# Attention followed by a learned density, one core: the density's last product moved from VectorE to ScalarE and POOL, with new pacing and a reordered tail

## The chip, the cores and the metric

The kernel runs on one core of one Trainium2 chip. Its time is device microseconds of that core. A core has TensorE (PE; its weight loads are listed apart as PEld), VectorE (DVE), ScalarE (ACT), GpSimd (POOL) and SyncE (SP, which issues DMAs). Each engine executes its own queue in order; a waiting instruction holds up all that stand behind it on the same engine.

## What is computed

The input `x` has 8 images of 192 channels and 64 x 64 pixels, in float32. Two layers follow each other, each added to its input. Both normalize first: the mean and variance of each group of 6 channels over all pixels of an image.

```python
# layer 0: attention over the 4096 pixels of an image
q = prelu(conv1x1(x, w1, b1), a1)        # 24 channels
k = prelu(conv1x1(x, w2, b2), a2)        # 24 channels
v = prelu(conv1x1(x, wa, ba), aa)        # 192 channels
score = softmax(einsum('bnc,bcm->bnm', q, k), axis=2)
out = einsum('bnm,bmc->bnc', score, v)
# layer 1: a small network for each channel, widths 1, 3, 3, 3, 1
for i in range(4):
    logits = einsum('cij,cjn->cin', softplus(ms[i]), logits) + bs[i]
    if i < 3:
        logits = logits + tanh(fs[i]) * tanh(logits)
# lower and upper are these logits for x - 0.5 and x + 0.5
sign = -sign(lower + upper)
likelihood = max(abs(sigmoid(sign * upper) - sigmoid(sign * lower)), 1e-6)
```

The density of an image (layer 1) can begin only when the attention output of that whole image is there, since its norm is taken over all of it.

## The kernel before

**The loop.** The attention of all images is one stream of 1,024 steps, 128 for an image: 8 blocks of 512 queries (`n`), and 16 steps of 256 keys each in a block. In a step TensorE makes the scores of the next step (L780), the products from which the row maximum of a later block is taken (L708, 22 steps ahead), and adds `e` times `v` to the block's accumulator (L795). ScalarE takes the exponential (L784), VectorE reduces the maximum (L716). At the end of a block the accumulator is divided, transposed through the tiles `o` and added to `xc` (`finish`, L806 to L840); after the last block of an image its norm follows (`norm_end`), a chain of small products and small VectorE instructions that ends in `wn` and `bn` (L503, L506).

**Beside it.** Keys, queries and values of the next image are made by jobs that take free steps; `keys` (L609) writes both keys and queries to a tile `kq`, from which two DMAs take them away. The density of an image runs beside the attention of the next one.

**The density.** It is cut into 12 units for an image: 2 column parts `c`, 3 channel groups `g`, and `s` for lower and upper. A unit works on tiles of 128 x 1,024 in 17 shared buffers `d`. ScalarE makes tanhs (L1005 of the input, L1020 later ones) and the first term of each sum, with scale and bias (L1014, L1030); VectorE adds each further term by one instruction that multiplies by a number per partition and adds (L1037): 9 "mixes" into layer 1, 3 gates, 6 products of layer 2, 3 gates, and 2 products of the last layer, 23 in all. When both units of a pair (`c`, `g`) are done, `ending` (L1135) makes the likelihood and adds it to `xc`: in the loop with POOL (L1160, L1172, L1180, each on half the columns), near the end on VectorE alone (`alone`, L1187 to L1197), then the absolute value (L1205), the sum (L1209) and the stores (L1213).

**The order.** It is written out by a planner while the program is built. A step `t` is a slot in all queues; `at(t, fn)` puts work into a later slot. In each slot `density_step` (L1086) gives VectorE, ScalarE and TensorE a credit and lets the oldest three units issue instructions as long as there is credit, inputs were issued earlier, and enough buffers stay for older units (`need`, L1063). VectorE's credit per step in the loop is the work left, divided by the steps until 15 after the next image's end. `pool_step` (L1120) issues one POOL piece in a step, behind a one-column memset (`pause`, L1125) that waits for the last but one density product of VectorE, so that the piece starts near the reduce.

**The tail.** The density of the last image has no attention beside it. There the nine mixes and the linear terms of a unit go to TensorE, for all units but the first: for each of three outputs, 8 matmuls of 512 columns against diagonal matrices (L978) add up in PSUM; ScalarE takes the tanh from there (L986) and VectorE gates it (L996). The diagonals (27 from weights at L876, 9 from the norm at L882) are made by ScalarE after the loop. After the loop each slot has a credit of 4.15.

Of the kernel before, what the change touches and what calls it, by code (L numbers as in the profile page):

```python
# [9 lines left out]
F32 = mybir.dt.float32  # L10
# [7 lines left out]
def kernel(  # L18
# [590 lines left out]
    def keys(b, d, what, done):  # L609

        t = xi[what, b, d]
        c, h = divmod(d, 2)
        i = c % 2

        def make(pk, u):
            if b not in kt:
                kt[b] = kpool.tile([128, N // 4], F32, tag="k", name=f"k_{b}")
            write, read = spotted()
            for g in range(3):
                write(nc.tensor.matmul(  # L620
                    pk[:, 0:P], lhsT=wf[i, b][:, g, :], rhs=t[:, g, :],
                    start=g == 0, stop=g == 2,
                ))
            done()
            kq = work.tile([128, P], F32, tag="kq", bufs=3, name=f"kq_{b}_{d}")
            first, last = prelu(
                None, kq, pk[:, 0:P], wf["b", i, b], nslope[:, i : i + 1],
                [x[:, 0:P] for x in u], read,
            )

            def move():
                last()
                k, q = (slice(64 * j, 64 * j + 64) for j in (i, 1 - i))
                u = (c // 2) * F + h * P
                nc.sync.dma_start(out=kt[b][k, u : u + P], in_=kq[k])
# [170 lines left out]
    def finish(b, n, t):  # L806
        a = acc.pop((b, n))
        rc = small.tile([128, 4], F32, tag="rc", name=f"rc_{b}_{n}")
        o = [
            work.tile([128, 3, 2, R], F32, tag=f"o{k}", name=f"o{k}_{b}_{n}") for k in range(2)  # L810
        ]
        cell = {}

        def invert():
            nc.vector.reciprocal(rc, a[:, :, C])

        def evacuate(k):
# [14 lines left out]

        u = slice((n % 4) * 256, (n % 4) * 256 + 256)

        def residual():
            xcc = xc[b, n // 4]
            nc.vector.tensor_tensor(xcc[:, :, u], xcc[:, :, u], cell["po"][:, 0:3, :], ALU.add)

            at(now[0] + 1, stat, 1.3)

        def stat():
            for g in range(3):
                norm_stat((b, 1), 3 * n + g, xc[b, n // 4][:, g, u])
            if n == NB - 1:
                norm_end((b, 1), 3 * NB, now[0] + 1, lambda: density(b))

        def make(po, _):
            cell["po"] = po.rearrange("p a (j c) -> p (a j) c", j=2)
            return [(0, turn, 0.0, 0.0, 1.3), (1, residual, 1.0, 0.0, 0.0)]
# [12 lines left out]

    ACT_RATE = 2.9
    OTHER = 0.1
    COST = {"DVE": 1.22, "ACT": 1.23, "TANH": 1.05, "PE": 6.95}
    diag = []
    banks = deque()
    lower2 = mm.rearrange("p g n -> p (g n)")[:, 0:36].rearrange("p (s g i) -> p s g i", s=4, g=3)

    def diagonals(g):  # L870

        d = vtiles.pop(0).rearrange("p a b c -> p (a b c)")[:, 0 : 12 * 128]
        d = d.rearrange("p (k n) -> p k n", k=12)
        diag.append(d)
        for k in range(9):
            nc.scalar.activation(d[:, k, :], ident, AF.Copy, scale=lc[:, g, k : k + 1])  # L876

    def linear_diagonals(b):
        wn, bn = norms[b, 1]
        for g in range(3):  # L880
            for i in range(3):
                nc.scalar.activation(  # L882
                    diag[g][:, 9 + i, :], ident, AF.Copy, scale=wn[:, g, 1, i : i + 1]
                )

        for s in range(2):
            d, q = lower2[:, s], lower2[:, 2 + s]
# [14 lines left out]
    class Unit:  # L902
# [3 lines left out]
        def __init__(self, b, c, g, s):  # L906
# [1 line left out]
            self.at = {}  # L908
            self.buf = {}
            self.todo = {"DVE": deque(), "ACT": deque(), "PE": deque()}  # L910
            self.left = {"l": 6, "t": 9, "u": 0, "z": 1}
            self.held = {"l": 0, "t": 0, "u": 0, "z": 0}
            self.on_pe = b == B - 1 and c + g + s > 0
            add = self.add
            if self.on_pe:

                self.left.update(t=3, u=3)
                for i in range(3):
                    add("ACT", ("u", 0, i), [], self.tanh0, makes="u")
                for i in range(3):  # L920
# [25 lines left out]
            for i in range(3):  # L946
                add("DVE", ("gate", 2, i), [("t", 2, i)], self.gate, frees=[("t", 2, i)])
            add("ACT", ("l", 3, 0), [("gate", 2, 0)], self.scaled, makes="z")
            for j in (1, 2):
                add("DVE", ("add", 3, 0, j), [("gate", 2, j), ("l", 3, 0)], self.more)  # L950

        def add(self, eng, name, after, fn, makes=None, frees=()):
            self.todo[eng].append((name, after, fn, makes, frees))
# [95 lines left out]
        def more(self, k):  # L1049
# [4 lines left out]
                for q in range(3):  # L1054
                    self.give(("l", 1, q))
            if (n, j) == (3, 2):
                for q in range(3):
                    self.give(("l", 2, q))
                b, c, g, s = self.key
                if not any(u.key == (b, c, g, 1 - s) and u.todo["DVE"] for u in units):  # L1060
                    ending(b, c, g)

        def need(self):  # L1063
            most = dict(self.left, t=max(0, min(self.left["t"], 1 - self.held["t"])))
            return sum(most.values())

        def step(self, eng, t, older):
# [18 lines left out]
    def density_step(t, rate):  # L1086
        if units and t < last:

            left = sum(len(u.todo["DVE"]) for u in units if u.key[0] == units[0].key[0])
            rate = left * COST["DVE"] / max(1, (units[0].key[0] + 2) * IMG + 15 - t) + OTHER  # L1090
        act = ACT_RATE if t < last else rate

        for eng, most in (("DVE", rate), ("ACT", act)):
# [1 line left out]
            credit[eng] = min(credit[eng] + most, most + more)  # L1095
        credit["PE"] = min(credit["PE"] + rate, rate)
        for eng in ("ACT", "PE", "DVE"):
            order = list(range(min(3, len(units))))
            if len(units) == 2:

                order.sort(key=lambda n: -len(units[n].todo["DVE"]))
            for n in order:
                units[n].step(eng, t, list(units)[:n])
        for u in [u for u in units if not u.todo["DVE"]]:
            units.remove(u)

    def density(b):
        if b == B - 1:
            linear_diagonals(b)
        for c in range(2):  # L1110
            for g in range(3):
                for s in range(2):
# [22 lines left out]
    def ending(b, c, g):  # L1135
# [46 lines left out]
        def alone():  # L1182

            s = cell["s"]

            def first():
                nc.vector.tensor_tensor(s, z[0], z[1], ALU.add)  # L1187
                later(1, second, 0.0, 2.1)

            def second():  # L1190
                for i in range(2):
                    nc.scalar.activation(z[i], z[i], AF.Tanh, scale=0.5)
                later(1, third, 2.5)

            def third():
                nc.vector.tensor_tensor(z[0], z[1], z[0], ALU.subtract)
                nc.vector.scalar_tensor_tensor(z[0], s, 0.0, z[0], ALU.not_equal, ALU.mult)  # L1197
                bufs.extend((s, z[1]))
                later(1, size, 0.0, 1.1)
                later(2, store, 1.3)  # L1200

            later(1, first, 1.25)

        def size():
            nc.scalar.activation(z[0], z[0], AF.Abs, scale=0.5)  # L1205

        def store():
            x_ = xc[b, c][:, g, :]
            nc.vector.scalar_tensor_tensor(x_, z[0], 1e-6, x_, ALU.max, ALU.add)  # L1209
            bufs.append(z[0])  # L1210
            for i in range(2):
                k = i * N // 2 + c * 2 * F
                nc.sync.dma_start(  # L1213
                    out=ov[b, :, g, k : k + 2 * F], in_=x_[R * i : R * i + R]
                )
            if g == 2:
                xc.pop((b, c))
                free["xc"] += 1
# [135 lines left out]
    for t in range(last):  # L1354
        b = t // IMG
        if t % IMG == 0:
            within(b, t)
            if b + 1 < B:
                prepare(b + 1, t)
        now[0] = t  # L1360
        if t % STEPS == 0:
            homes[:] = [(turns[(t // STEPS + 1) % 2], [0, 0])]
# [8 lines left out]
        work_off(t, RATE - 1.215)  # L1371
    t = last
    homes[:] = [(turns[1], [0, 0])]
    for g in range(3):
        at(t + 4 + g, lambda g=g: diagonals(g))
    while due or units or jobs or loads:
        work_off(t, RATE)
        t += 1
# [1 line left out]

# [36 lines left out]
```

## Time and profile before

| | us |
|---|---|
| median of 3 runs | 4846.51 (4843.33 to 4850.05) |
| the profiled execution | 4845.56 |
| its span, first to last instruction | 4843.8 |
| busy: PE / PEld / DVE / ACT / POOL | 4656.6 / 3443.8 / 4260.6 / 3116.6 / 523.3 |

The page's groups of instructions, with the count, busy time, mean ns of one and the idle time before it:

```profile
L716 DVE TENSOR_REDUCE rm<-mx 128x1 f32<-128x1024 f32 x1002 | 1222.4, 1220 | 445.9 <-PE mx L708 440.8
L1037 DVE SCALAR_TENSOR_TENSOR d<-d,wsp,d 128x1024 f32<-128x1024 f32 x768 | 984.6, 1283 | 45.7 <-ACT d L1030 34.4
L1160 POOL TENSOR_TENSOR d<-d,d 128x512 f32<-128x512 f32 x80 | 173.1, 2164 | 0.7 <-issue 0.2
```

A busy time is a sum over the whole span and says nothing about which engine sets the pace of a stage; a busy TensorE is busy in the records also where its matmuls wait inside the pipeline. VectorE's large instructions have a mean of about 1.28 us, but the next one starts 1.2 us after: their ends overlap. The chain of work that ended last runs over PE for 79% of the span and over DVE for 14%.

### The profile page before, as it was taken

The page shows a single profiled execution, that of the slowest core. Times are in us where ns is not written, and L with a number is a line of the kernel's source. Part 1 is how long each engine was busy: PE and PEld are TensorE (multiplying, and loading weights), DVE is VectorE, ACT ScalarE, POOL GpSimd, SP SyncE. Part 2 cuts the span into 40 slices and gives each one's busy share as a digit, 9 for nine tenths or more (in the row PEclk, how much of TensorE's full clock was granted, in tenths as well). Part 3 has the DMA queues.
Part 4 walks back from the last instruction along what each step waited for, and adds up shares of the span by engine and source line. Part 5 has one row for each costly group of instructions (what it writes and reads, how often), then busy time and mean ns, then how long its engine had stood idle before and what let it go on. Part 6 is the DMA issues. An engine that isn't in the chain of part 4 may idle for free.

```text
span 4843.8 us, 68352 instructions
## 1 busy us (share of the span) xinstructions
PE 4656.6 (96%) x28384; PEld 3443.8 (71%) x28384; DVE 4260.6 (88%) x4378; ACT 3116.6 (64%) x3581; POOL 523.3 (11%) x506
## 2 busy tenths in 40 slices
PE   7999999999999999999999999999999999999496
PEld 5777777777777777777777777777777777777132
DVE  5433369999999999999999999999999999998887
ACT  2332247676767667777667766776777767777665
POOL 0000001111112111111111101111111111211000
PEclk9999999999999999999999999999999999999698
DMA  2101010001100111111110111110111100000000
GB/s 61 38 23 24 18 48 25 25 24 40 42 20 24 40 35 34 31 32 29 38 29 26 37 39 29 31 37 15 35 42 28 27 24 22 10 23 5 9 13 13
DMA packets 109163, 138.55 MB, mean 29 GB/s; under 512 B 17074, under 2 KB 82100, under 8 KB 108852
## 3 DMA queue, kind: packets, MB, share of 16 engines
q1 hardware_dynamic: 107616, 133.81, 11.0%
q8 instruction: 222, 3.64, 0.3%
q14 instruction: 89, 0.73, 0.1%
q10 hardware_dynamic: 1236, 0.37, 0.0%
HBM read 100.58 MB, written 29.36 MB: 27 GB/s over the span
## 4 chain that ended last, share of the span: by engine, by line
PE 79%; DVE 14%; ACT 4%; issue 1%; POOL 1%; DMA 0%; ACTq 0%; DVEq 0%; POOLq 0%
PE b L795 48%; PE sc L780 18%; DVE d L1037 9%; PE b L669 4%; DVE rm L716 3%; PE b L978 2%; PE b L620 1%; PE sc_tail L978 1%; PE mx_tail L978 1%; PE b L828 1%; ACT e L784 1%; PE mx L708 1%; ACT d L1005 1%; ACT d L1030 1%; ACT d L1020 1%
## 5 line engine op out<-in xcount | busy, mean ns | idle before, releaser
L795 PEld LDWEIGHTS b<-v,e 128*128 128x128 f32 x16384 | 2662.2, 191 | 779.1 <-issue 775.3
L795 PE MATMUL b<-v,e 128*128 128x193 f32 x16384 | 2966.5, 335 | 0.0
L784 ACT ACTIVATE e<-sc 128x1024 f32<-128x1024 f32 x1024 | 1044.9, 1020 | 1444.1 <-PE mx L708 1409.3
L716 DVE TENSOR_REDUCE rm<-mx 128x1 f32<-128x1024 f32 x1002 | 1222.4, 1220 | 445.9 <-PE mx L708 440.8
L780 PE MATMUL sc<-q,k 25*128 25x512 f32 x4096 | 1155.8, 640 | 22.4 <-ACT e L784 22.3
L708 PE MATMUL mx<-k,q 24*128 24x512 f32 x4008 | 1132.7, 641 | 14.1 <-DVE rm L716 13.8
L1037 DVE SCALAR_TENSOR_TENSOR d<-d,wsp,d 128x1024 f32<-128x1024 f32 x768 | 984.6, 1283 | 45.7 <-ACT d L1030 34.4
L1037 DVE SCALAR_TENSOR_TENSOR d<-d,lc,d 128x1024 f32<-128x1024 f32 x765 | 986.5, 1300 | 16.5 <-ACT d L1014 5.1
L1037 DVE SCALAR_TENSOR_TENSOR d<-d,tf,d 128x1024 f32<-128x1024 f32 x543 | 680.9, 1277 | 2.5 <-ACT d L1020 2.5
L1020 ACT ACTIVATE d<-d 128x1024 f32<-128x1024 f32 x543 | 568.0, 1053 | 65.3 <-DVE d L1037 64.7
L780 PEld LDWEIGHTS sc<-q,k 25*128 25x128 f32 x4096 | 306.4, 183 | 249.9 <-issue 189.1
L1125 POOL MEMSET pause<- 128x1 f32 x240 | 23.5, 98 | 3888.0 <-DVE d L1037 3888.0
L1030 ACT ACTIVATE d<-d,cb,wsp 128x1024 f32<-128x1024 f32 x351 | 433.4, 1235 | 2.3 <-DVE d L1037 1.7
L1005 ACT ACTIVATE d<-xc,bn,wn 128x1024 f32<-128x1024 f32 x288 | 353.6, 1234 | 12.2 <-DVE bn L506 11.4
L708 PEld LDWEIGHTS mx<-k,q 24*128 24x128 f32 x4008 | 299.9, 183 | 30.3 <-DVE rm L716 29.1
L1014 ACT ACTIVATE d<-xc,bn,wn 128x1024 f32<-128x1024 f32 x255 | 314.7, 1234 | 0.0
L1160 POOL TENSOR_TENSOR d<-d,d 128x512 f32<-128x512 f32 x80 | 173.1, 2164 | 0.7 <-issue 0.2
L1172 POOL TENSOR_TENSOR d<-d,d 128x512 f32<-128x512 f32 x80 | 167.3, 2092 | 0.4 <-issue 0.4
L1180 POOL TENSOR_TENSOR d<-d,d 128x512 f32<-128x512 f32 x80 | 161.7, 2021 | 1.9 <-ACT d L1030 0.3
L669 PE MATMUL b<-wv,xi 64*128 64x192 f32 x1344 | 139.5, 340 | 0.2 <-ACT pra L596 0.2
L669 PEld LDWEIGHTS b<-wv,xi 64*128 64x128 f32 x1344 | 106.5, 186 | 25.7 <-issue 20.2
L978 PE MATMUL b<-d,v 128*128 128x512 f32 x204 | 95.9, 622 | 17.1 <-ACT d L1005 17.1
(154 smaller groups left out, 2064.4 us busy)
## 6 DMA issues: line engine op xcount, KB each, us to landing
xi<-in_x_dram SPq DMA_DIRECT2D x280, 192.0 KB, 3.4
xc<-in_x_dram SPq DMA_DIRECT2D x64, 384.0 KB, 7.0
out_dram<-xc SPq DMA_DIRECT2D x96, 256.0 KB, 3.1
q<-qd SPq DMA_DIRECT2D x128, 128.0 KB, 2.6
k<-kq SPq DMA_DIRECT2D x64, 64.0 KB, 1.9
qd<-kq SPq DMA_DIRECT2D x64, 64.0 KB, 2.1
d<-in_x_dram SPq DMA_DIRECT2D x16, 192.0 KB, 4.6
d<-in_wat_dram ACTq DMA_DIRECT2D x2, 144.0 KB
```

The lines of the kernel that those rows point to most:

```text
L669: nc.tensor.matmul(pv[:, s, 0:C], lhsT=t[p, g, k * 128 : k * 128 + 128] if g < 3 else one_row[p], rhs=wf["v", b][p, g, :] if g < 3 else wf ...
L708: nc.tensor.matmul(sc[:, s, :], lhsT=tile_of(qt[b, n // 2], n, j)[r], rhs=kt[b][r, u : u + F], start=True, stop=True,)
L716: nc.vector.tensor_reduce(out=rowmax[b, n][:, j, k : k + 1], in_=sc, axis=AX.XY, op=ALU.max)
L780: nc.tensor.matmul(sc[:, s, :], lhsT=kt[b][r, k : k + 128], rhs=qt[b, n // 2][r, :, u : u + 256], start=True, stop=True,)
L784: return lambda: nc.scalar.activation(e, sc, AF.Exp)
L795: nc.tensor.matmul(a[:, j, 0 : C + 1], lhsT=e[:, s, j * 128 : j * 128 + 128], rhs=v[:, s, p % 4, :], start=p == 0 and s == 0 and j % 2 == ...
L978: nc.tensor.matmul(out[:, h, :], lhsT=diag[g][:, 3 * i + n - 1 if n else 9 + i, :], rhs=src[:, h * F : h * F + F], start=n == 0, stop=n == 3,)
L1005: nc.scalar.activation(self.buf[k], self.src(), AF.Tanh, bias=bn[:, s, g, 0, i : i + 1], scale=wn[:, g, 0, i : i + 1],)
L1014: nc.scalar.activation(self.buf[k], self.src(), AF.Identity, bias=bn[:, s, g, 1, i : i + 1], scale=wn[:, g, 1, i : i + 1],)
L1020: nc.scalar.activation(self.buf[k], self.buf["l", k[1], k[2]], AF.Tanh)
L1030: nc.scalar.activation(self.buf[k], self.buf["l", n - 1, 0], AF.Identity, bias=offset, scale=wsp[:, g, w : w + 1],)
L1037: nc.vector.scalar_tensor_tensor(dst, src, factor, dst, ALU.mult, ALU.add)
```

## The change

1. In units that do not use TensorE (now all units of the first seven images), the last layer's last product, `("add", 3, 0, 2)` on VectorE, becomes a copy with a scale on ScalarE into a buffer of its own (`plain`, kind `p`), and two POOL pieces that add its halves to the unit's result.
2. The credit of VectorE in the loop has a ceiling `MOST` of 3.3.
3. `need` counts the buffers of the last layer only when the second layer's last product has been issued.
4. `kq` goes from three buffers to two; the tiles `o` from one to two each.
5. The tail: the weights' diagonals are made one by one in the last steps of the loop; the norm's diagonals are spread over slots; until the last norm is there a slot's credit is 1.3; after the loop up to four units may issue; the first unit uses TensorE too; the last pair's ending works on halves and stores halves.

```diff
-            kq = work.tile([128, P], F32, tag="kq", bufs=3, name=f"kq_{b}_{d}")
+            kq = work.tile([128, P], F32, tag="kq", bufs=2, name=f"kq_{b}_{d}")
...
-            work.tile([128, 3, 2, R], F32, tag=f"o{k}", name=f"o{k}_{b}_{n}") for k in range(2)
+            work.tile([128, 3, 2, R], F32, tag=f"o{k}", bufs=2, name=f"o{k}_{b}_{n}") for k in range(2)
...
+    MOST = 3.3
...
-    def diagonals(g):
-
-        d = vtiles.pop(0).rearrange("p a b c -> p (a b c)")[:, 0 : 12 * 128]
-        d = d.rearrange("p (k n) -> p k n", k=12)
-        diag.append(d)
+    def diagonals(g, t):
+
+        def one(k):
+            if k == 0:
+                d = vtiles.pop(0).rearrange("p a b c -> p (a b c)")[:, 0 : 12 * 128]
+                diag.append(d.rearrange("p (k n) -> p k n", k=12))
+            nc.scalar.activation(diag[g][:, k, :], ident, AF.Copy, scale=lc[:, g, k : k + 1])
+
         for k in range(9):
-            nc.scalar.activation(d[:, k, :], ident, AF.Copy, scale=lc[:, g, k : k + 1])
+            at(t + k, lambda k=k: one(k), 0.0, 0.4)
...
-            self.on_pe = b == B - 1 and c + g + s > 0
+            self.on_pe = b == B - 1
...
-            for j in (1, 2):
-                add("DVE", ("add", 3, 0, j), [("gate", 2, j), ("l", 3, 0)], self.more)
+            add("DVE", ("add", 3, 0, 1), [("gate", 2, 1), ("l", 3, 0)], self.more)
+            if self.on_pe:
+                add("DVE", ("add", 3, 0, 2), [("gate", 2, 2), ("l", 3, 0)], self.more)
+            else:
+
+                add("ACT", ("p", 3, 2), [("gate", 2, 2), ("add", 3, 0, 1)], self.plain, makes="p")
...
+        def plain(self, k):
+            g = self.key[2]
+            src, dst, z = self.buf["l", 2, 2], self.buf[k], self.buf["l", 3, 0]
+            nc.scalar.activation(dst, src, AF.Copy, scale=wsp[:, g, 23:24])
+
+            def add(h):
+                n = slice(h * F, h * F + F)
+                if h == 1:
+                    at(now[0] + 1, lambda: self.give(k))
+                return nc.gpsimd.tensor_tensor(z[:, n], z[:, n], dst[:, n], ALU.add)
+
+            pieces.append(lambda: add(0))
+            pieces.append(lambda: add(1))
+            self.end()
...
         def need(self):
             most = dict(self.left, t=max(0, min(self.left["t"], 1 - self.held["t"])))
+            if ("add", 2, 2, 2) not in self.at:
+
+                most.update(z=0, p=0)
             return sum(most.values())
...
             rate = left * COST["DVE"] / max(1, (units[0].key[0] + 2) * IMG + 15 - t) + OTHER
+            rate = min(rate, MOST)
...
-            order = list(range(min(3, len(units))))
-            if len(units) == 2:
+            order = list(range(min(3 if t < last else 4, len(units))))
+            if len(units) == 2 and t < last:
...
         if b == B - 1:
-            linear_diagonals(b)
+            linear_diagonals(b, 0)
+            for g in (1, 2):
+                at(now[0] + 3 * g, lambda g=g: linear_diagonals(b, g), 0.0, 1.2)
+            at(now[0] + 1, lambda: tail(b), 2.2)
...
+            parts = halves if (b, c, g) == (B - 1, 1, 2) else [slice(0, 2 * F)]
...
+                diagonals(0, t + 93)
+                diagonals(1, t + 104)
+                diagonals(2, last - 11)
...
-    for g in range(3):
-        at(t + 4 + g, lambda g=g: diagonals(g))
     while due or units or jobs or loads:
-        work_off(t, RATE)
+
+        work_off(t, RATE if (B - 1, 1) in norms else 1.3)
         t += 1
```

More of the change, by code (lines that the diff above doesn't have):

```diff
@@ L868, with linear_diagonals, tail @@
     lower2 = mm.rearrange("p g n -> p (g n)")[:, 0:36].rearrange("p (s g i) -> p s g i", s=4, g=3)
-    def diagonals(g):
-        d = vtiles.pop(0).rearrange("p a b c -> p (a b c)")[:, 0 : 12 * 128]
-        d = d.rearrange("p (k n) -> p k n", k=12)
-        diag.append(d)
+    def diagonals(g, t):
[4 more added lines that the diff above has]
+            nc.scalar.activation(diag[g][:, k, :], ident, AF.Copy, scale=lc[:, g, k : k + 1])
         for k in range(9):
-            nc.scalar.activation(d[:, k, :], ident, AF.Copy, scale=lc[:, g, k : k + 1])
-    def linear_diagonals(b):
+            at(t + k, lambda k=k: one(k), 0.0, 0.4)
+    def linear_diagonals(b, g):
         wn, bn = norms[b, 1]
-        for g in range(3):
[L881 to L884, printed above, removed]
+        for i in range(3):
+            nc.scalar.activation(
+                diag[g][:, 9 + i, :], ident, AF.Copy, scale=wn[:, g, 1, i : i + 1]
+            )
+    def tail(b):
+        wn, bn = norms[b, 1]
         for s in range(2):
@@ L910, in __init__ @@
             self.todo = {"DVE": deque(), "ACT": deque(), "PE": deque()}
-            self.left = {"l": 6, "t": 9, "u": 0, "z": 1}
-            self.held = {"l": 0, "t": 0, "u": 0, "z": 0}
-            self.on_pe = b == B - 1 and c + g + s > 0
+            self.left = {"l": 6, "t": 9, "u": 0, "z": 1, "p": 1}
+            self.held = {"l": 0, "t": 0, "u": 0, "z": 0, "p": 0}
+            self.on_pe = b == B - 1
             add = self.add
             if self.on_pe:
-                self.left.update(t=3, u=3)
+                self.left.update(t=3, u=3, p=0)
                 for i in range(3):
@@ L1056, in more, with end, busy @@
             if (n, j) == (3, 2):
[L1057 to L1061, printed above, removed]
+                self.end()
[10 more added lines that the diff above has]
+            pieces.append(lambda: add(1))
+            self.end()
+        def end(self):
+            for q in range(3):
+                self.give(("l", 2, q))
+            b, c, g, s = self.key
+            if not any(u.key == (b, c, g, 1 - s) and u.busy() for u in units):
+                ending(b, c, g)
+        def busy(self):
+            return self.todo["DVE"] or self.todo["ACT"]
         def need(self):
             most = dict(self.left, t=max(0, min(self.left["t"], 1 - self.held["t"])))
+            if ("add", 2, 2, 2) not in self.at:
+                most.update(z=0, p=0)
             return sum(most.values())
@@ L1103, in density_step @@
                 units[n].step(eng, t, list(units)[:n])
-        for u in [u for u in units if not u.todo["DVE"]]:
+        for u in [u for u in units if not u.busy()]:
             units.remove(u)
@@ L1184, in alone @@
             s = cell["s"]
+            parts = halves if (b, c, g) == (B - 1, 1, 2) else [slice(0, 2 * F)]
             def first():
-                nc.vector.tensor_tensor(s, z[0], z[1], ALU.add)
+                for n in parts:
+                    nc.vector.tensor_tensor(s[:, n], z[0][:, n], z[1][:, n], ALU.add)
                 later(1, second, 0.0, 2.1)
             def second():
-                for i in range(2):
-                    nc.scalar.activation(z[i], z[i], AF.Tanh, scale=0.5)
+                for n in parts:
+                    for i in range(2):
+                        nc.scalar.activation(z[i][:, n], z[i][:, n], AF.Tanh, scale=0.5)
@@ L1193, in second @@
                 later(1, third, 2.5)
             def third():
-                nc.vector.tensor_tensor(z[0], z[1], z[0], ALU.subtract)
-                nc.vector.scalar_tensor_tensor(z[0], s, 0.0, z[0], ALU.not_equal, ALU.mult)
+                for n in parts:
+                    y = z[0][:, n]
+                    nc.vector.tensor_tensor(y, z[1][:, n], y, ALU.subtract)
+                    nc.vector.scalar_tensor_tensor(y, s[:, n], 0.0, y, ALU.not_equal, ALU.mult)
                 bufs.extend((s, z[1]))
-                later(1, size, 0.0, 1.1)
@@ L1200, in third, with size @@
-                later(2, store, 1.3)
+                later(1, lambda: size(parts), 0.0, 1.1)
+                later(2, lambda: store(parts), 1.3)
             later(1, first, 1.25)
[L1204 to L1209, printed above, removed]
-            bufs.append(z[0])
[L1211 to L1215, printed above, removed]
+        def size(parts=(slice(0, 2 * F),)):
+            for n in parts:
+                nc.scalar.activation(z[0][:, n], z[0][:, n], AF.Abs, scale=0.5)
@@ L1216, in store @@
+        def store(parts=(slice(0, 2 * F),)):
+            for n in parts:
+                x_ = xc[b, c][:, g, n]
+                nc.vector.scalar_tensor_tensor(x_, z[0][:, n], 1e-6, x_, ALU.max, ALU.add)
+                for i in range(2):
+                    k = i * N // 2 + c * 2 * F
+                    nc.sync.dma_start(
+                        out=ov[b, :, g, k + n.start : k + n.stop], in_=x_[R * i : R * i + R]
+                    )
+            bufs.append(z[0])
             if g == 2:
@@ L1359 @@
                 prepare(b + 1, t)
+            else:
+                diagonals(0, t + 93)
+                diagonals(1, t + 104)
+                diagonals(2, last - 11)
         now[0] = t
@@ L1373 @@
     homes[:] = [(turns[1], [0, 0])]
-    for g in range(3):
-        at(t + 4 + g, lambda g=g: diagonals(g))
     while due or units or jobs or loads:
-        work_off(t, RATE)
+        work_off(t, RATE if (B - 1, 1) in norms else 1.3)
         t += 1
```

## The prediction

> **What bounds the kernel now.** I read the page first, then a table of windows by image and for the tail, then the timeline where the table showed a loss. In the windows the columns after the length are the busy times of TensorE, its weight load, VectorE, ScalarE and POOL, each with a count, then the granted clock, the DMA share and GB/s.
>
> ```profile
> 88.90:632.00 543.10, 540.85 (x3458) 410.39 (x3456) 202.02 (x280) 163.89 (x214) 0.00 (x0) 1.00 0.10 25
> 1737.50:2293.90 556.40, 551.84 (x3484) 417.35 (x3482) 541.04 (x549) 392.40 (x452) 78.08 (x72) 0.99 0.13 32
> 4479.50:4531.30 51.80, 2.78 (x11) 2.14 (x10) 49.92 (x59) 33.35 (x56) 0.00 (x0) 0.53 0.04 10
> 4531.30:4586.70 55.40, 34.24 (x65) 14.21 (x66) 49.26 (x54) 42.09 (x45) 0.00 (x0) 0.76 0.04 10
> 4586.70:4807.30 220.60, 204.34 (x465) 88.28 (x463) 178.60 (x146) 141.84 (x132) 0.00 (x0) 0.98 0.04 10
> 4807.30:4843.80 36.50, 0.00 (x0) 0.00 (x0) 25.92 (x22) 14.05 (x13) 0.00 (x0) 0.54 0.11 29
> ```
>
> The first row is image 0's attention, with no density beside it: 543.1 us, TensorE full. The second is image 3's, with image 2's density: 13 us longer, and VectorE now full too (541 of 556). The loop's floor is TensorE. Timing the loop by the first score matmul of each step, a plain step takes 3.88 us (median and minimum of 675), one with value products 5.38, with keys 5.18, with the output transposes 4.54. The medians sum to 4,301 us; the real steps take **84 us more**: 1.6, 6.2, 13.6, 13.6, 13.2, 13.0, 13.0 and 9.9 us in images 0 to 7. That is all the loop can give back. Some 10 us of each 13 lie in steps 13 to 17, where the old density's due time, the new norm and the next image's statistics meet:
>
> ```profile
> 1809.08 2.67 DVE L1037 SCALAR_TENSOR_TENSOR d<-d,lc,d 128x1024 f32<-128x1024 f32 x2
> ...
> 1811.66 1.22 DVE L716 TENSOR_REDUCE rm<-mx 128x1 f32<-128x1024 f32 x1
> ...
> 1812.94 1.69 PE L708 MATMUL mx<-k,q 24*128 24x512 f32 x4 [2.77 <-DVE rm L716]
> ...
> 1814.56 5.52 PE L795 MATMUL b<-v,e 128*128 128x193 f32 x16
> ```
>
> VectorE reached this reduce late, TensorE stood 2.77 us, and its next 16 matmuls took 5.52 us where they usually take 2.88: the records show the granted clock at 0.5 from 1813.4 to 1820.2. Being late costs twice.
>
> The tail, from 4479.5 on, has four stages: norm of the last image (VectorE busy 49.9 of 51.8), start of TensorE's products, the steady products, the drain. The span ends 1.8 us inside the profiled 4845.56, which is 0.95 under the median.
>
> **The last product (84 units of images 0 to 6).** Removed: 84 L1037 instructions; two in a row take 2.60, so 1.2 start to start, 101 us in all or 14.4 per image. Added on ScalarE: 84 copies with a scale; not in the trace, between L1020 (1.05) and L1030 (1.24), I take 1.15 (two operands, no bias): 14 us an image, under ScalarE's 164 us of idle time an image. Exposed, it would cost those 14. Added on POOL: 168 half adds behind 168 pauses, 24 per image. Their price is the open question, since the adds can hold up VectorE:
>
> ```profile
> 1822.46 2.60 DVE L1037 SCALAR_TENSOR_TENSOR d<-d,lc,d 128x1024 f32<-128x1024 f32 x2
> ...
> 1823.91 2.27 POOL L1160 TENSOR_TENSOR d<-d,d 128x512 f32<-128x512 f32 x1
> ...
> 1825.19 1.22 DVE L716 TENSOR_REDUCE rm<-mx 128x1 f32<-128x1024 f32 x1
> ...
> 4410.14 2.21 POOL L1180 TENSOR_TENSOR d<-d,d 128x512 f32<-128x512 f32 x1
> ...
> 4411.14 3.61 DVE L1037 SCALAR_TENSOR_TENSOR d<-d,wsp,d 128x1024 f32<-128x1024 f32 x2
> ```
>
> In the first case the half add waits out the second product and then runs beside the reduce: both DVE rows keep their usual length. In the second no reduce follows, and two products take 3.61, 1.0 more. The Trainium skill ("SBUF — State Buffer", Who interferes with whom) says the shared port pair is an exclusive lock: a VectorE instruction with two SBUF inputs and a GpSimd one that reads SBUF block each other wholly. By that rule alone all 168 adds collide at 1.0 each, 168 us against 101 saved: the change would lose. The row decides, as the pause puts the add beside a reduce: over all 240 half adds of the trace the L1037 durations above 1.28 sum to 20 us, and VectorE's idle time inside POOL's spans to 22.5, so 0.08 to 0.18 each. I take 0.1: 2.4 us an image.
>
> **Ceiling, later counting, order.** These only move instructions; the changed program's order shows how. In steps 8 to 19 of images 3 to 6 stand 28 instructions of 1,024 columns on VectorE before, 21 after. Before: 28 x 1.2, 12 reduces x 1.14, 10 statistics x 0.5 and small ones of 4.4 make 56.7 us, against 47.2 of TensorE; after, 48.3. The nearest rows are image 1 (17 instructions, 43.5 us), which lost 4.4 us in these steps, and image 7 (49.9 us), which lost 4.8; so 4.7 is what I expect, the norm chain and ScalarE's burst after it staying. With 1.8 elsewhere, images 2 to 7 lose 6.5 each, image 1 4.5, image 0 1.6: 45 instead of 84. **Loop: -39 us** (ends: -70, nearly all gone; -10, only the light steps gain).
>
> **Buffers.** `kq` with two buffers: in the prologue eight writes come 1.3 us apart and each buffer's second DMA lands 2.1 after issue, so the third write waits: +1.5 us (0 to 3). In the loop the writes are 3.9 us or more apart: nothing. Second `o` buffers: the old ones were free for 16 steps: nothing.
>
> **The tail.** Four edits act together. The norm chain now stands behind far fewer products:
>
> ```profile
> 4496.75 0.95 DVE L837 TENSOR_TENSOR xc<-xc,b 128x768 f32<-128x768 f32 x1
> ...
> 4505.71 5.12 DVE L1037 SCALAR_TENSOR_TENSOR d<-d,wsp,d 128x1024 f32<-128x1024 f32 x4 [0.34 <-ACT d L1030]
> 4510.75 0.15 DVE L462 COPY nrm<-b 128x2 f32<-128x2 f32 x1
> ...
> 4531.03 0.38 DVE L506 SCALAR_TENSOR_TENSOR bn<-wx,nmr,bx 128x18 f32<-128x18 f32 x2
> ```
>
> The small copy at 4510.75 waited behind four products. Before, 37 large instructions stand between the last reciprocal and `bn`; after, 11. Counted after the last attention: evacuation behind seven ScalarE instructions +7; transposes (1.54) +8.5; residual behind four large ones and two tanhs +12; store, statistics, aggregate +15.3; mean product, one product, small ones +17.4; variance, two products +20.5; table load and root, two products, the rest +24. Before: 51.8. So 28 us earlier (ends: ready at +20 or +35). The 27 diagonals (7.98 us of ScalarE at 4493) move under the loop, free there.
>
> But the work only moves: after `bn` VectorE has about 268 us of it instead of 249 (the image 6 leftover, less nine mixes of the first unit, 10.8 us), and TensorE has 36 products instead of 33. Product 4 ended 55.4 us after the norm, because its third tanh0 stands on ScalarE behind tanhs that wait for VectorE; it stands there still, with what is ahead some 5 us earlier: +50. The other products came every 220.6/29 = 7.6 us, close to TensorE's own 6.87 per product; the steady order on ScalarE and VectorE is the same afterwards. So 24 + 50 + 32 x 7.6 + drain 31.7, less 2 for the ending in halves = 347, against 359.5 before. **Tail: -12 us** (ends: -35 if the early gap also closes, +10 if `bn` comes at +35 and products at 8.0). The final half stores replace two DMAs by four small ones: nothing on balance.
>
> Sum: -39 + 1.5 - 12 = -50 on 4845.56, 4796 profiled, near 4796 in the median.
>
> **Rivals.**
> *More is freed* (4747): the stall in the crowd goes wholly, with its clock drops (loop -70), and TensorE's early gap too (tail -30). For it: VectorE's new total of 525 an image leaves 18 us. Against: lighter images 1 and 7 stall too.
> *The crowd stays* (4826): the norm chain and the ScalarE burst set the stall, not the count (loop -10, tail -10). For it: image 1, at 504 us of VectorE, still lost 6.2.
> *The tail does not do what it says* (4817): `bn` waits on ScalarE and on POOL's adds, now ahead of it, until +40, and three more products cost their 22.8: tail +9.
> *POOL's lock* (slower, about 4900): pieces rise from 36 to 60 per 128 steps; if adds no longer find a reduce and cost 1.0, an image gets 24 against 14.4 us, +9.6 on an engine already full, 67 over seven, less 12 in the tail. It decides from 0.6 us per half add. Against: one piece a step, each paused.
>
> **Chances.** Forecast 0.60, more freed 0.13, crowd stays 0.14, tail fails 0.08, POOL's lock 0.05. The range 4762 to 4828 leaves out the POOL case and half of the case of more freed. A measurement tells 0.2% (10 us, 4837) from no change; faster than that are the first four cases but for their edges.
>
> **What would show it.** Right: loop losses of 5 to 7 us in images 2 to 7; L1037 durations unchanged beside POOL; `bn` 24 us after the last attention; products still 7.6 apart. Wrong: L1037 at 2.3 us in mid-loop (POOL), steps 13 to 17 still losing 10 us (crowd), `bn` later than +35, or a TensorE without the gap ahead of product 4.

## The result and the profile after

The changed kernel takes **4799.99 us** (median of 3 runs, 4798.78 to 4801.53) against 4846.51: ratio 0.9904, 95% interval 0.9882 to 0.9926. Its profiled execution took 4801.53 us, its span 4799.7.

The page's groups first, with the columns as before:

```profile
L716 DVE TENSOR_REDUCE rm<-mx 128x1 f32<-128x1024 f32 x1002 | 1222.3, 1220 | 481.4 <-PE mx L708 472.7
L708 PE MATMUL mx<-k,q 24*128 24x512 f32 x4008 | 1130.4, 640 | 0.6 <-DVE rm L716 0.6
L1047 DVE SCALAR_TENSOR_TENSOR d<-d,wsp,d 128x1024 f32<-128x1024 f32 x684 | 883.3, 1292 | 53.1 <-ACT d L1040 44.7
L1078 POOL TENSOR_TENSOR d<-d,d 128x512 f32<-128x512 f32 x168 | 331.8, 1975 | 47.7 <-ACT d L1072 46.6
L1198 POOL TENSOR_TENSOR d<-d,d 128x512 f32<-128x512 f32 x80 | 173.0, 2163 | 0.0
```

The 84 products are gone from VectorE (768 to 684) and stand on POOL as 168 half adds. The mean of a VectorE product is nearly what it was. TensorE's wait for a late reduce (L708 behind L716) is 0.6 us, the clearest single sign in the loop. In the kernel before its list of waits (total us, times, longest) had:

```profile
PE mx L708 <- DVE rm L716: 13.8, 5, 2.8
```

The windows, for image 0, image 3 and the tail up to `bn`, up to the last product, and to the end:

```profile
91.90:636.60 544.70, 542.45 (x3454) 411.26 (x3452) 201.99 (x280) 164.01 (x214) 0.00 (x0) 0.99 0.10 25
1734.90:2284.80 549.90, 545.89 (x3488) 414.18 (x3486) 531.51 (x537) 404.50 (x464) 123.90 (x120) 1.00 0.14 32
4445.20:4470.50 25.30, 2.74 (x11) 2.13 (x10) 18.25 (x32) 15.72 (x19) 1.78 (x3) 0.54 0.08 21
4470.50:4766.50 296.00, 257.73 (x576) 110.68 (x576) 253.67 (x219) 198.03 (x190) 9.05 (x8) 0.96 0.04 9
4766.50:4799.70 33.20, 0.00 (x1) 0.00 (x0) 22.88 (x23) 12.36 (x14) 0.00 (x0) 0.58 0.13 32
```

Image 3 takes 549.9 us instead of 556.4. The loop starts 3.0 us later (91.9 against 88.9) and its last attention ends at 4445.2 instead of 4479.6. `bn` comes 25 us after that instead of 52. But from `bn` to the last product it is now 296.0 us where it was 276.1, for three products more. The tail, from the last attention to VectorE's last instruction, is 349.7 us against 359.4: most of what the early norm brought has gone again.

Timed by the first score matmul of each step as in the prediction, the losses over TensorE's floor are, by image:

| | 0 | 1 | 2 | 3 | 4 | 5 | 6 | 7 | all |
|---|---|---|---|---|---|---|---|---|---|
| before | 1.6 | 6.2 | 13.6 | 13.6 | 13.2 | 13.0 | 13.0 | 9.9 | 84.2 |
| after | 3.3 | 4.3 | 8.3 | 7.1 | 7.1 | 7.1 | 7.1 | 2.9 | 47.1 |

The clock records go with this. In images 1 to 7 they show half clock nine times before, 37.5 us in all, and twice after, 6.8 us. If TensorE does half as much in such a stretch, that is some 15 of the 37 us (an estimate from these lengths).

Of the 7.1 us that image 3 still loses, 3.1 lie in steps 8 to 19 and 1.9 in steps 24 and 25. Those two are of another kind, as the timeline shows:

```profile
1836.34 1.00 ACT L784 ACTIVATE e<-sc 128x1024 f32<-128x1024 f32 x1
1837.35 1.28 ACT L484 ACT_TABLE_LOAD   x1
1837.38 0.70 PE L780 MATMUL sc<-q,k 25*128 25x512 f32 x2 [0.73 <-ACT e L784]
...
1840.00 1.28 ACT L784 ACT_TABLE_LOAD   x1
...
1842.37 0.70 PE L780 MATMUL sc<-q,k 25*128 25x512 f32 x2 [1.03 <-ACT e L784]
```

TensorE waits for the exponential, which is late on ScalarE: the first time behind density work, the second time also behind the two table loads of a square root. VectorE is not what holds these two steps up.

So the sum was met. Whether the reasons were, only single parts can tell.

### The profile page after: what moved, and what is told of

The parts are those of the page before. It is cut to its first block, busy times and chain, and to the rows that moved or that the text cites. A ratio compares the mean times of both kernels' runs of the same rounds, so it can differ in the third digit from the quotient of the medians.

```text
span 4799.7 us, 69014 instructions
## 1 busy us (share of the span) xinstructions
PE 4653.4 (97%) x28432; PEld 3440.0 (72%) x28432; DVE 4179.0 (87%) x4289; ACT 3196.8 (67%) x3665; POOL 856.3 (18%) x842
## 4 chain that ended last, share of the span: by engine, by line
PE 86%; DVE 7%; ACT 5%; issue 1%; DMA 0%; POOL 0%; ACTq 0%; SPq 0%; DVEq 0%; POOLq 0%
PE b L795 53%; PE sc L780 20%; PE b L669 4%; DVE d L1047 4%; PE b L988 2%; PE b L620 2%; DVE rm L716 1%; ACT d L1015 1%; ACT e L784 1%; PE mx_tail L988 1%; PE sc_tail L988 1%; PE b L828 1%; PE mx L708 1%; ACT d L1040 1%; PE b L745 0%
## 5 line engine op out<-in xcount | busy, mean ns | idle before, releaser
L716 DVE TENSOR_REDUCE rm<-mx 128x1 f32<-128x1024 f32 x1002 | 1222.3, 1220 | 481.4 <-PE mx L708 472.7
L708 PE MATMUL mx<-k,q 24*128 24x512 f32 x4008 | 1130.4, 640 | 0.6 <-DVE rm L716 0.6
L1047 DVE SCALAR_TENSOR_TENSOR d<-d,lc,d 128x1024 f32<-128x1024 f32 x756 | 986.1, 1314 | 12.2
L1047 DVE SCALAR_TENSOR_TENSOR d<-d,wsp,d 128x1024 f32<-128x1024 f32 x684 | 883.3, 1292 | 53.1 <-ACT d L1040 44.7
L1163 POOL MEMSET pause<- 128x1 f32 x408 | 40.0, 98 | 3613.2 <-DVE d L1047 3613.2
L1078 POOL TENSOR_TENSOR d<-d,d 128x512 f32<-128x512 f32 x168 | 331.8, 1975 | 47.7 <-ACT d L1072 46.6
L708 PEld LDWEIGHTS mx<-k,q 24*128 24x128 f32 x4008 | 299.8, 183 | 7.3 <-DVE rm L716 6.7
L1198 POOL TENSOR_TENSOR d<-d,d 128x512 f32<-128x512 f32 x80 | 173.0, 2163 | 0.0
L1210 POOL TENSOR_TENSOR d<-d,d 128x512 f32<-128x512 f32 x80 | 163.2, 2040 | 0.5 <-issue 0.5
L1218 POOL TENSOR_TENSOR d<-d,d 128x512 f32<-128x512 f32 x80 | 157.6, 1970 | 2.5 <-POOL pause L1163 0.9
```

The costliest lines, as they stand in the source:

```text
L708: nc.tensor.matmul(sc[:, s, :], lhsT=tile_of(qt[b, n // 2], n, j)[r], rhs=kt[b][r, u : u + F], start=True, stop=True,)
L716: nc.vector.tensor_reduce(out=rowmax[b, n][:, j, k : k + 1], in_=sc, axis=AX.XY, op=ALU.max)
L1047: nc.vector.scalar_tensor_tensor(dst, src, factor, dst, ALU.mult, ALU.add)
L1078: return nc.gpsimd.tensor_tensor(z[:, n], z[:, n], dst[:, n], ALU.add)
```

## Which part makes the gain: five runs

**The ceiling alone.** The kernel before, and one line:

```diff
+            rate = min(rate, 3.3)
```

> The kernel before with the ceiling of 3.3 alone, nothing else. Its order has 24 large VectorE instructions in steps 8 to 19 of images 3 to 6 (51.9 us of work) where before has 28 (56.7 us) and after 21 (48.3 us); the work per image stays at 539 us. My theory (the loop's loss follows the crowd in these steps): losses of images 2 to 6 fall from 13.3 to about 8.7, the loop gives 23 us, time near 4823. Rival (the loss follows VectorE's total work per image, so only the moved product helps): no change, 4843 to 4848.

Measured: 4815.39 us against 4848.5 of before in the same comparison, ratio 0.9935 (0.992 to 0.995). The loop's loss is 54.5 us instead of 84.2; image 3 as a window:

```profile
1729.40:2280.30 550.90, 547.04 (x3487) 415.72 (x3485) 537.91 (x549) 392.23 (x453) 79.65 (x72) 1.00 0.13 32
```

VectorE does all the work that it did before (538 us, 541 before) and the image takes 550.9 us instead of 556.4. With the amount of work unchanged, a more even order alone takes away 30 of the loop's 84 us. The theory's direction is right and its size too small: 33 us where 23 were expected.

**The move without the ceiling.** The kernel after, less the ceiling and the later counting:

```diff
-            rate = min(rate, MOST)
...
-            if ("add", 2, 2, 2) not in self.at:
-
-                most.update(z=0, p=0)
```

> The kernel after without the ceiling and without the later counting: the moved last product, the buffers and the new tail stay. VectorE's work per image is the low 525 us, as after, but the order puts 30 large instructions into steps 8 to 19 (59.1 us). My theory: the crowd decides, so the loop loses as much as before or more (84 to 95 us), only the tail's 10 us are gained: 4836 to 4848. Rival (total work decides): as after, 4800 to 4806.

Measured: **4888.63 us**, ratio 1.0088 (1.0071 to 1.0104): slower than before by 40 us, although VectorE has less to do. The loop loses 134 us, 22 to 23 in each of images 2 to 6. Image 3 as a window, and its step 18 in the timeline:

```profile
1749.80:2314.50 564.70, 555.23 (x3488) 419.70 (x3486) 528.67 (x538) 403.43 (x464) 125.52 (x120) 0.99 0.13 32
```

```profile
1822.97 8.89 DVE L1047 SCALAR_TENSOR_TENSOR d<-d,lc,d 128x1024 f32<-128x1024 f32 x7
...
1831.78 1.22 DVE L716 TENSOR_REDUCE rm<-mx 128x1 f32<-128x1024 f32 x1
...
1833.05 2.07 PE L708 MATMUL mx<-k,q 24*128 24x512 f32 x4 [5.07 <-DVE rm L716]
...
1835.05 4.75 PE L795 MATMUL b<-v,e 128*128 128x193 f32 x16
```

Seven products stand ahead of one reduce (five ahead of the late one in the kernel before, of which the prediction's view shows the last two). TensorE stands still for 5.07 us, and the matmuls after it run at half clock for a while: 4.75 us where 2.88 is usual, the clock at 0.5 from 1832.1 to 1838.9. VectorE is busy 529 of 565 us: less than before, and the image is 8 us longer. Total work does not decide; the rival falls. Even the crowd theory expected at most 4848, so it priced a crowd of 30 too low. Half clock is part of it (71.7 us of such stretches in images 1 to 7, 37.5 before); the rest was not taken apart.

**The tail alone.** The kernel after with the last product on VectorE, without ceiling and later counting; what stays are the tail and the buffers.

```diff
-            if self.on_pe:
-                add("DVE", ("add", 3, 0, 2), [("gate", 2, 2), ("l", 3, 0)], self.more)
-            else:
-
-                add("ACT", ("p", 3, 2), [("gate", 2, 2), ("add", 3, 0, 1)], self.plain, makes="p")
+            add("DVE", ("add", 3, 0, 2), [("gate", 2, 2), ("l", 3, 0)], self.more)
```

> The kernel before with only the new tail and the buffer counts: last product on VectorE, no ceiling, old counting. My theory: tail -10, prologue +3, loop within 3 of before: 4836 to 4842; norm ready some 25 us after the last attention. Rival (the tail's gain comes from the work that the moved product took away from its start): no gain, 4846 to 4852.

Measured: 4833.21 us, ratio 0.9968 (0.9956 to 0.998), a little better than the range. The loop loses 87.1 us, about as before, so the second `o` buffers give it nothing. It starts 4.2 us later; the tail is 342.1 us, 17 less than before and 7.6 less than in the kernel after.

**Everything but the move.** The same edit as a diff, with ceiling and later counting kept.

> The kernel after with the last product back on VectorE: ceiling, later counting, buffers and new tail stay. 24 large VectorE instructions in steps 8 to 19 (51.9 us), as with the ceiling alone, which lost 54.5 us in the loop. Theory A (the ceiling makes nearly the whole loop gain, the move only trims the crowd): loop loss near 55 against 47, tail as after: 4805 to 4812. Theory B (the move itself frees the loop, as the prediction had it with its 14.4 us per image): loop loss back to 70 or more, 4822 to 4840.

Measured: 4804.94 us (4799.41 to 4809.03) against 4849.95, ratio 0.9909 (0.9894 to 0.9924), beside 0.9904 (0.9882 to 0.9926) of the kernel after. The profiled loop lost 63.8 us, 16.7 more than after, and its tail was 340.9 us, 8.8 less; that execution was the slowest of its four. The change's headline, the last product moved off VectorE, is worth 5 us by the medians and 2.5 by the ratios, well inside the intervals of the two: these runs do not separate it from zero. Without it the rest gives 45 of the 46.5 us. The ceiling alone (33.1 us) and the tail alone (15.3) also add up to about the whole.

**Only the ceiling taken away.**

```diff
-            rate = min(rate, MOST)
```

> The kernel after without the ceiling alone; later counting, the moved product and the new tail stay (the run of the move without ceiling lacked both). 23 large VectorE instructions in steps 8 to 19 of image 3 (50.7 us), where that run had 30. Theory (what matters is the crowd that the order makes, and the later counting clears most of it): loop loss 50 to 58, 4802 to 4812. Rival (the ceiling is what the move needs): 4840 or more.

Measured: 4806.42 us, ratio 0.9913 (0.9898 to 0.9928), loop loss 59.5: the theory's range. So the later counting clears the crowd that the move makes also without the ceiling; it is without both that the move costs. The later counting is worth 82 us here (4888.63 against 4806.42). By itself without the move, or the ceiling without it beside the move, was not tried.

**The crowd, counted.** The traces of these runs, and of the last one below, can be laid side by side. The table has VectorE's instructions of 1,024 columns in steps 8 to 19, and what these steps lose over TensorE's floor, as a mean of images 3 to 6:

| run | last product | instructions | us lost |
|---|---|---|---|
| nine buffers, ceiling at 2.9 | moved | 18 | 0.5 |
| after | moved | 21 | 3.1 |
| no ceiling | moved | 23 | 6.4 |
| ceiling alone | on VectorE | 24 | 4.4 |
| everything but the move | on VectorE | 24 | 4.4 |
| before | on VectorE | 28 | 10.6 |
| move without ceiling and later counting | moved | 30 | 15.1 |

Apart from 23 and 24, which stand in the wrong order, the loss follows the count, whether the last product is moved or not. The count is not all: image 1, with 16 or 17 of them, still loses about 4 us in these steps in every run.

## What a half add on POOL costs

The kernel after, with POOL's pieces no longer held back:

```diff
-            if len(recent) == 2:
-                inst = nc.gpsimd.memset(pause, 0.0)
-                tc.add_manual_dep(
...
             pieces.popleft()()
```

> The kernel after with POOL's pieces no longer paced by the memset that waits for VectorE: the same 408 half adds, free to start whenever their inputs are there. If the pause is what keeps their price at 0.1 us (my theory), the adds now meet products and cost VectorE 0.3 to 1.0 each, 120 to 400 us over seven images with some 100 us of room: 4830 to 5000, with many L1047 instructions of about 2.2 us. Rival (the lock is short in any place): within 5 us of after, 4795 to 4805.

Measured: **4942.33 us**, ratio 1.0195 (1.018 to 1.0211), 142 us above the kernel after. From the timeline of this kernel:

```profile
1965.17 4.41 POOL L1078 TENSOR_TENSOR d<-d,d 128x512 f32<-128x512 f32 x2 [37.57 <-ACT d L1072]
...
1966.14 2.30 DVE L1047 SCALAR_TENSOR_TENSOR d<-d,tf,d 128x1024 f32<-128x1024 f32 x1
...
1969.50 1.59 DVE L599 SCALAR_TENSOR_TENSOR kq<-prb,nslope,prb 128x256 f32<-128x256 f32 x1
1969.54 2.69 POOL L1189 TENSOR_TENSOR d<-d,d 128x512 f32<-128x512 f32 x2
```

The product takes 2.30 us instead of 1.28, and `kq`, 0.5 in the prologue, 1.59. The page's group of the mixes tells it for the whole run (mean 1,454 ns; 1,314 in the kernel after):

```profile
L1047 DVE SCALAR_TENSOR_TENSOR d<-d,lc,d 128x1024 f32<-128x1024 f32 x756 | 1091.8, 1454 | 12.2
```

Summing what VectorE's products last beyond 1.29 us and dividing by the 408 half adds: 0.08 before (of 240 adds), 0.11 after, 0.54 without the pause. These rows agree with the Trainium skill's rule of the exclusive lock ("SBUF — State Buffer", Who interferes with whom): the product is longer by 1.02 us, most of the 1.25 that a free half add lasts. The pause of 0.1 us on POOL is what keeps this cheap. In the kernel after, 301 of the 408 adds start while a product is running, wait it out (2.15 us in the median, 1.25 at the least) and go on beside a reduce, and no reduce lasts more than 1.23 us. Without the pause only 106 do; many of the others meet a further product, which then is the one that waits. Of the products that lie beside an add for 0.9 us or more, 38 of 339 last over 1.5 us with the pause and 237 of 287 without.

At 0.54 the 168 half adds of the move would cost 91 us (an estimate), nearly all of the 101 that it takes off VectorE (84 products of 1.2), close to the 0.6 that the prediction worked out as the turning point.

## What sets the tail

**The norm's place.** The kernel after with the old credit ahead of the norm:

```diff
-        work_off(t, RATE if (B - 1, 1) in norms else 1.3)
+        work_off(t, RATE)
```

> The kernel after with the old credit of 4.15 in the slots before the last norm instead of 1.3. The norm chain then stands behind more VectorE products; bn should come 40 to 52 us after the last attention instead of 25.5. My theory (TensorE's 36 products follow the norm one by one, so a later norm moves the end, save what the early gap of 28 us before the fifth product gives back): 8 to 25 us slower, 4808 to 4825. Rival (the work only changes places): within 4 of after.

Measured: 4803.08 us, ratio 0.9907 (0.989 to 0.9923): the rival. `bn` came 50.1 us after the last attention instead of 25.5, and the tail was 351.2 us instead of 349.7. The windows of this kernel, up to `bn`, to the last product, to the end:

```profile
4443.40:4493.30 49.90, 2.73 (x11) 2.15 (x10) 46.05 (x54) 27.62 (x30) 6.29 (x7) 0.52 0.04 11
4493.30:4766.10 272.80, 252.12 (x576) 108.86 (x576) 223.09 (x196) 186.04 (x179) 2.64 (x4) 0.99 0.04 10
4766.10:4799.40 33.30, 0.01 (x1) 0.00 (x0) 22.89 (x23) 12.39 (x14) 0.00 (x0) 0.56 0.13 32
```

The 24.6 us that the norm comes earlier in the kernel after come back as 23.2 us more between `bn` and the last product. They come back nearly all in one place. TensorE in the kernel after, at its fourth product:

```profile
4497.50 1.88 PE L988 MATMUL mx_tail<-xc,v 128*128 128x512 f32 x4
4502.62 5.10 PE L988 MATMUL mx_tail<-d,v 128*128 128x512 f32 x8 [3.25 <-ACT d L1015]
4521.96 3.78 PE L988 MATMUL mx_tail<-d,v 128*128 128x512 f32 x4 [14.24 <-ACT d L1015]
```

It waits 14.24 us for the third tanh0 of the second unit, and the fifth product starts 28.0 us after the fourth; with the late norm it starts 6.9 us after.

**The first unit.** Back to VectorE for its mixes, 33 products instead of 36:

```diff
-            self.on_pe = b == B - 1
+            self.on_pe = b == B - 1 and c + g + s > 0
```

> The kernel after with the first unit of the last image on VectorE again (its nine mixes), 33 products on TensorE instead of 36. If the tail is set by TensorE's products, 7.5 us apart (my theory): three fewer, less some waiting on 10.8 us more of VectorE: 10 to 20 us less, 4780 to 4790. Rival (VectorE sets the tail): 5 to 11 us more, 4805 to 4812.

Measured: 4797.47 us, ratio 0.9894 (0.9879 to 0.9909), between the two theories. Three products fewer gave no 20 us: the second product came 53.3 us after the first. The tail followed neither the count of products nor VectorE's work.

**Buffers.** Three value tiles, free after the last attention, join the shared buffers:

```diff
     t = last
     homes[:] = [(turns[1], [0, 0])]
+    for v in vtiles:
+        bufs.append(v.rearrange("p a b c -> p (a b c)")[:, 0 : 2 * F])
```

> The kernel after with three of the value tiles, free once the last attention is done, added to the shared buffers d for the tail. If the fifth product's 28 us gap comes from the planner's wait for buffers (the second unit's third tanh0 has none until the older units give some back), it shrinks, and the steady 8.9 us steps with it: 10 to 25 us less, 4775 to 4790. Rival (the gap is VectorE's backlog from image 6, or ScalarE's order): within 4 of after, 4796 to 4804.

Measured: 4783.71 us, ratio 0.9865 (0.985 to 0.9879). The 28.0 us before the fifth product became 7.2; a gap of 21.4 us came before the eighth. So the wait was for buffers: the planner lets a young unit take one only if enough stay for the older ones, and so puts its tanh0 late into ScalarE's queue.

**Three units.** The kernel after with the old limit and order:

```diff
-            order = list(range(min(3 if t < last else 4, len(units))))
-            if len(units) == 2 and t < last:
+            order = list(range(min(3, len(units))))
+            if len(units) == 2:
```

> The kernel after with at most three units issuing in the tail and the old sorting of the last two. If the fourth unit and the unsorted order are what shortens the tail (the earlier norm was shown to give nothing by itself), the tail is 5 to 15 us longer: 4805 to 4815. Rival (the tail's gain is the drain in halves, 3.3 us, and small things): within 4 of after.

Measured: 4786.05 us, ratio 0.9873 (0.9858 to 0.9888), 14 us **better** than the kernel after: the expectation had the wrong sign. The gap before the fifth product is 14.1 us instead of 28.0, the tail 336.4 us. A fourth unit that takes buffers while the first three wait for them fits this; that it is the buffers here, and not the order, was not shown apart.

**Nine buffers.** The run with three spare buffers, and beside the value tiles also the last two key, query and exponential tiles:

```diff
+    exs = deque(maxlen=2)
...
+        exs.append(e)
...
+    for e in (kt[B - 1], kt[B - 2], qt[B - 1, NC - 1], qt[B - 1, NC - 2], *exs):
+        bufs.append(e if len(e.shape) == 2 else e.rearrange("p s n -> p (s n)"))
```

> As the run with three spare value tiles, with six more buffers that are free after the last attention (two each of keys, queries and exponentials). If buffers still hold the tail (a gap of 21.4 us before its eighth product, steps of 7 to 10 us), that goes: TensorE's 36 products at 6.9 and VectorE's 268 us after bn are the bounds: 4758 to 4778. Rival (VectorE's backlog makes the rest): within 4 of the run with three, 4780 to 4788.

Measured: 4759.13 us, ratio 0.9816 (0.98 to 0.9832). From `bn` to the last product, and the drain:

```profile
4467.70:4720.40 252.70, 249.59 (x576) 109.64 (x576) 245.04 (x214) 193.44 (x187) 8.60 (x8) 0.99 0.04 11
4720.40:4756.90 36.50, 0.03 (x1) 0.00 (x0) 28.71 (x28) 15.38 (x17) 0.00 (x0) 0.55 0.12 29
```

TensorE is busy 249.6 of 252.7 us and VectorE 245.0: products start 6.9 us apart nearly throughout, and the tail is 310.0 us. Only now is the tail set by what the prediction took for its pace.

**And a lower ceiling.** The same with the ceiling at 2.9:

```diff
-    MOST = 3.3
+    MOST = 2.9
```

> As the run with nine spare buffers, with the ceiling at 2.9 instead of 3.3: 18 large VectorE instructions in steps 8 to 19 of images 3 to 6 (44.7 us) where after has 21 (48.3 us), the rest pushed into later steps. If the crowd on VectorE is what still loses: another 5 to 12 us off the run with nine buffers. Rival (what is left in these steps is ScalarE, table loads and exponentials late): within 4 of it.

Measured: **4744.18 us** (4743.63 to 4746.15), ratio 0.9786 (0.9771 to 0.98): the fastest, 106 us below before and 56 below the change. The loop loses 29.5 us, 3.2 in each of images 3 to 6. The gain of 15 us over nine buffers alone is more than expected; the part of the crowd on VectorE that was left was still worth that.

## Why the prediction was right, and where it was right for another reason

- **Sum and sign.** 4796 forecast, 4799.99 measured; -44 us in the profiled executions, -50 forecast.
- **The loop.** -39 forecast, -37.1 measured (84.2 to 47.1). Steps 13 to 17 as the place, and the count of VectorE's instructions in steps 8 to 19 as the measure, are borne out by the table of the crowd. 6.5 us for each of images 2 to 7 were forecast; 8.3, four times 7.1 and 2.9 came. Inside that sum two errors met, which is luck: steps 8 to 19 lost 3.1 us in images 3 to 6 where 4.7 were expected, and the other steps 4.0 where 1.8 were, in part because ScalarE is now late in steps 24 and 25. The text put the moved product first, with 14.4 us per image; by the runs the order gives nearly all of it, and the move next to nothing. Its 1.2 us from start to start is the median of successive products, but the pair of 2.60 from which it was read starts 1.31 apart.
- **POOL.** 0.1 us per half add was right (0.11), and because of the pause: without it 0.54. The text set the Trainium skill's rule against the row, but they don't differ: the rule is about VectorE instructions with two inputs in SBUF, and the reduce has one, in PSUM. So the rule never said that all 168 adds collide.
- **The prologue.** +3.0 us instead of +1.5, the upper end. The wait forecast is there: VectorE stands 5.3 us, in three writes, for the DMA that empties `kq`. In the ceiling alone, with three `kq` buffers, the loop began at 88.9 as before; in the other runs with two it began at 89.5 to 93.1, so the term varies between executions.
- **The norm.** +24 forecast, +25.5 measured, along the chain of steps given. But "28 us earlier" was not a gain: undone, it cost 1.5 us in the tail. The step that failed is the one after it, "it stands there still, with what is ahead some 5 us earlier: +50". The fourth product ended 54.8 us after `bn`, as late as before (55.4). Its third tanh0 does stand on ScalarE behind tanhs that wait for VectorE, but it was put there by the planner, which held back buffers: with three more of them the fifth product starts 7.2 us after the fourth. The other terms came out near: products 7.53 us apart (7.6 forecast), a drain of 28.4 (29.7). The tail's sum is met, and the reason for which the early norm was to pay is not.
- **What the tail's 9.7 us are made of.** The drain is 3.3 of them (31.7 to 28.4), presumably by the halves, which were not tried alone. The tail edits alone made the tail 17 us shorter. With ceiling and later counting it was 18.5 us shorter (340.9), and the move took 8.8 of that back. The fourth unit with its order costs 13 (349.7 against 336.4). How the rest divides among the earlier diagonals, the first unit and the norm was not taken apart.

## What to carry to other kernels

When an engine beside the bottleneck is nearly full on average, ask for its work step by step: in the move without the ceiling, reduces that came late made an image 8 us longer, although 12 us of VectorE's work had gone from it. When an early step is brought forward, look for what the next ones are waiting for; here it was buffers, which stood free under other names. Work moved to POOL was cheap here where it was held back until a reduce was next on VectorE, and five times as dear where it was not.

## What the runs showed of the hardware that was not expected

A short wait of TensorE can be followed by a stretch at half clock: after 2.77 us of standing, the records have 0.5 from 1813.4 to 1820.2 us in the kernel before; with the move and without ceiling and later counting there are stretches of 10.2 us in images 2 and 4. Not every wait does it, and the runs don't show from what length on. And a VectorE instruction of a single column was not exempt from POOL: in the kernel after, `rq` (L491, 128x1) took 1.17 us beside a half add, 0.16 elsewhere.
